# Layer 3's key tiles taken two at a time in one stream across blocks, with one mask product on GpSimd

## Chip, cores and metric

One core of one Trainium2 chip. The metric is the device time of one execution in microseconds (us), lower is better.

## The reference, cut to what matters

Four residual layers on a tensor of 4 images, 256 channels, 48 x 48 pixels. The change touches the last one only, a linear attention over three box windows (half sizes 24, 12 and 6 pixels):

```python
    def _L3_conv_ref(x, Wq, Wk, Wv, Wout, bout):      # HEADS = 8, WINDOWS = (1, 2, 4)
        ...
        q = jax.nn.sigmoid(q)
        k = jax.nn.sigmoid(k)
        v = v / jnp.maximum(jnp.linalg.norm(v, axis=1, keepdims=True), 1e-12)
        Ik = _integral(k)
        Ikv = _integral(jnp.einsum('bfhw,bghw->bfghw', k, v))
        outs = []
        for w in WINDOWS:
            ws = Hh // w
            wk = _box(Ik, ws, Hh, Ww)
            wkv = _box(Ikv, ws, Hh, Ww)
            attn = jnp.einsum('bdhw,bdfhw->bfhw', q, wkv)
            norm = jnp.einsum('bdhw,bdhw->bhw', q, wk)
            outs.append((attn / (norm[:, None] + 1e-06)).reshape(b, C, Hh, Ww))
        o = jnp.concatenate(outs, axis=1)
        return jnp.einsum('bchw,oc->bohw', o, Wout) + bout[None, :, None, None]
    ...
    x = x + _L3_conv_ref(_gn(x), L3_conv_Wq, L3_conv_Wk, L3_conv_Wv, L3_conv_Wout, L3_conv_bout)
```

## The kernel before

The kernel computes this as masked attention without a softmax. A **block** is one image, one pair of heads and 8 rows of queries (384 of them); there are 96. A **key tile** is 8 rows by 16 columns of keys; a block sees 12 to 18, in all 1440. For each tile TensorE makes the scores of both heads (two matmuls). For each of the three windows the scores are multiplied by a mask (VectorE; ScalarE copies the part where the mask is all ones) and TensorE adds them, times the values, to that window's sum. Such a **product** is one matmul call for each of the two heads, their 64-column weights side by side in the array, so that the heads can run at once; the trace shows each call as two instructions. Image 0's q, k and v are projected ahead of the stream of tiles; those of images 1 to 3 are dealt out between tiles by `background()`, as are the output projections.

```python
        def attend(b, ct, rb, pr, qs, background):
            accs = [ps_acc.tile(...) for wi in range(NW)]       # one PSUM buffer per window
            ...
            ahead = scores(*tiles[0])
            for i, (a, c) in enumerate(tiles):
                s = ahead
                if i + 1 < len(tiles):
                    ahead = scores(*tiles[i + 1])
                for wi in reversed(range(NW)):
                    if (a, c) not in todo[wi]:
                        continue
                    ...
                    for p0, p1, masked in pieces:               # the copied piece first, then the sides
                        if masked:
                            nc.vector.tensor_mul(dst, src, mask[wi][...])
                        else:
                            nc.scalar.copy(dst, src)
                    for j in range(2):                          # one product, head by head
                        nc.tensor.matmul(accs[wi][64 * j : 64 * (j + 1)]..., vst[pr][:, a * NKC + c, j, :],
                                         sm[:, j, 0:n, 0 : c1 - c0], start=..., stop=...)
                    if (a, c) == todo[wi][-1]:
                        nc.scalar.copy(stage[:, wi, :], accs[wi])
                background()
            ...                                                 # stores, on GpSimd's DMA queue
        ...
        for i, (b, ct, rb, pr) in enumerate(order):
            if (ct, rb, pr) == (0, 0, 0) and b + 1 < B:
                soon.append(projections(b + 1, ps_m, "st", [P, 512]))
            if i + 1 < len(order):
                qs[i + 1] = load_q(*order[i + 1])
            attend(b, ct, rb, pr, qs.pop(i), background)
            if rb == NRB - 1:                                   # the image's last blocks
                ...
                    while soon: ...                             # finish the next image's projections
                    load_kv(b + 1, 0, pr)
```

The order of instructions on an engine isn't that of this text: a scheduler decides it from the dependencies.

## Time and profile before

| | before |
|---|---|
| time, median (3 runs) | 4886.5 us (4876.69 to 4886.75) |
| span of the profiled run | 4876.6 us, mean granted clock 0.970 (the share of its full clock that TensorE was given) |
| image 0's projections, first matmul to first score of the stream | 1595.7 to 1709.7: 114.0 us |
| the stream of tiles, first score to the end of the last sum | 3124 us |
| last sum (its start) to the end | 43.3 us |
| busy over the whole span | TensorE 92%, VectorE 50%, ScalarE 22%, GpSimd 16% |

TensorE is nearly always busy, so the time is made in its own sequence: what its instructions need in this order, and where it waits. The other engines matter only by the waits they cause. The lines themselves stand in the prediction.

### The profile page before, as it was taken

What the parts mean: (1) busy time and instruction counts of PE and PEld (TensorE: products, weight loads), DVE (VectorE), ACT (ScalarE), POOL (GpSimd) and SP (SyncE); (2) the same over time, 40 slices, a digit from 0 to 9 for tenths busy, and PEclk for the clock granted to TensorE, in tenths of its full rate; (3) what the DMA queues carried; (4) which work ended last, traced back from release to release, by engine and by line L of the source; (5) the groups of instructions that cost most, each with busy time, mean ns of one, the idle gap of its engine ahead of it and who ended that gap; (6) DMA issues with size and microseconds to landing.
All of it is one profiled execution on the core that took longest, in us unless ns stands there. A gap on an engine that the chain in (4) does not pass through costs nothing.

```text
span 4876.6 us, 64267 instructions
## 1 busy us (share of the span) xinstructions
PE 4481.8 (92%) x24676; PEld 2571.1 (53%) x24676; DVE 2446.6 (50%) x5718; ACT 1088.2 (22%) x2227; POOL 756.9 (16%) x1237
## 2 busy tenths in 40 slices
PE   6999989989969699999999999999999998999997
PEld 4776967867858344444444444444444443444443
DVE  7543253253222155655555566555566565666564
ACT  0011001001010333223223322222322222322221
POOL 0000100100001732012123102212301211000111
PEclk9999999999979899999999999999999999999998
DMA  7241141141040641132252132234214225103222
GB/s 279 82 64 51 54 64 44 43 75 47 30 41 10 207 127 62 44 91 87 76 133 85 44 88 83 72 100 117 78 25 108 81 63 135 30 24 98 61 70 61
DMA packets 259252, 382.22 MB, mean 78 GB/s; under 512 B 96547, under 2 KB 207107, under 8 KB 252419
## 3 DMA queue, kind: packets, MB, share of 16 engines
q1 hardware_dynamic: 215267, 262.09, 20.1%
q0 software_dynamic: 38160, 108.02, 8.3%
q10 hardware_dynamic: 5520, 8.00, 0.5%
q8 instruction: 197, 3.23, 0.3%
q14 instruction: 108, 0.88, 0.1%
HBM read 259.50 MB, written 120.02 MB: 78 GB/s over the span
## 4 chain that ended last, share of the span: by engine, by line
PE 75%; DVE 9%; DMA 6%; issue 5%; POOL 3%; ACT 2%; SPq 1%; DVEq 0%; POOLq 0%; ACTq 0%
PE acc L1058 30%; PE s L1006 13%; PE cv L502 13%; PE cv L637 10%; DVE sm L1048 5%; PE out_ps L1120 4%; PE proj_ps L876 2%; PE ap L614 2%; POOL xn L862 1%; DVE o L1115 1%; DMA band_d<-e 1%; DMA rows<-band_d 1%; DMA nr<-n_d 1%; DVE v L458 1%; SPq L561 1%
## 5 line engine op out<-in xcount | busy, mean ns | idle before, releaser
L1048 DVE TENSOR_TENSOR sm<-s,masks 128x240 f32<-128x240 f32 (+22 forms) x4032 | 1688.5, 456 | 1118.0 <-PE s L1006 685.0
L1058 PE MATMUL acc<-sm,vst 128*64 128x320 f32 (+14 forms) x13440 | 1984.5, 398 | 122.8 <-DVE sm L1048 103.1
L1058 PEld LDWEIGHTS acc<-sm,vst 128*64 128x64 f32 x13440 | 761.7, 136 | 853.4 <-issue 405.5
L1056 ACT COPY sm<-s 128x528 f32<-128x528 f32 (+3 forms) x1440 | 690.7, 486 | 1603.3 <-DVE sm L1048 1586.7
L1006 PE MATMUL s<-qs,kst 128*128 128x320 f32 (+3 forms) x2880 | 838.0, 373 | 9.3 <-DVE sm L1048 8.6
L1006 PEld LDWEIGHTS s<-qs,kst 128*128 128x128 f32 x2880 | 435.3, 189 | 741.0 <-issue 693.1
L502 PE MATMUL cv<-v,wt 128*128 128x288 f32 x2912 | 763.4, 417 | 30.2 <-DVE v L458 21.0
L502 PEld LDWEIGHTS cv<-v,wt 128*128 128x128 f32 x2912 | 548.3, 192 | 195.6 <-issue 20.8
L637 PE MATMUL cv<-pad,wl_sb 128*128 128x384 f32 (+1 forms) x2592 | 476.8, 347 | 16.9 <-ACT pad L708 12.1
L637 PEld LDWEIGHTS cv<-pad,wl_sb 128*128 128x128 f32 x1728 | 322.6, 194 | 17.2 <-issue 12.3
L1072 POOL DMA_DIRECT2D o_d<-stage x192 | 97.0, 505 | 1314.2 <-ACT sm L1056 1059.5
L1120 PE MATMUL out_ps<-o,wout_sb 128*128 128x384 f32 x576 | 222.3, 513 | 45.2 <-DVE o L1115 44.4
L1068 ACT COPY stage<-acc 128x384 f32<-128x384 f32 x288 | 137.8, 478 | 483.4 <-PE acc L1058 477.1
L516 DVE SCALAR_TENSOR_TENSOR rows<-cv,rows 128x288 f32<-128x288 f32 x144 | 57.1, 450 | 284.2 <-PE cv L502 284.2
L1120 PEld LDWEIGHTS out_ps<-o,wout_sb 128*128 128x128 f32 x576 | 100.0, 191 | 139.4 <-DVE o L1115 66.8
L670 DVE SCALAR_TENSOR_TENSOR x<-cv,alpha,x 128x384 f32<-128x384 f32 x48 | 29.7, 618 | 224.3 <-PE cv L637 224.2
L446 POOL MEMSET v<- 128x192 f32 x28 | 8.3, 296 | 785.6 <-issue 416.5
L168 ACT ACTIVATE rsq_s<-gn_v 128x2 f32<-128x2 f32 x16 | 3.3, 204 | 561.1 <-DVE gn_v L195 561.1
L637 PEld LDWEIGHTS <-wl_sb 128*128 128x128 bf16 x864 | 85.9, 100 | 64.9 <-issue 7.7
L614 PEld LDWEIGHTS ap<-seen,xT 120*128 120x128 f32 (+2 forms) x832 | 105.6, 205 | 13.6 <-ACT seen L607 11.8
L181 DVE BATCH_NORM_STATS2 gn_st<-x 128x6 f32<-128x384 f32 x192 | 100.8, 552 | 23.7 <-DMA x<-in_x_dram 20.7
L614 PE MATMUL ap<-seen,xT 120*128 120x120 f32 (+3 forms) x832 | 109.7, 290 | 2.0 <-ACT seen L607 1.6
(145 smaller groups left out, 2197.9 us busy)
## 6 DMA issues: line engine op xcount, KB each, us to landing
qs<-q_d SPq DMA_DIRECT2D x384, 96.0 KB, 2.2
kst<-k_d SPq DMA_DIRECT2D x128, 288.0 KB, 7.8
wt<-wt SPq DMA_DIRECT2D x80, 448.0 KB, 3.9
o_d<-stage POOLq DMA_DIRECT2D x192, 144.0 KB, 2.3
o<-o_d POOLq DMA_DIRECT2D x24, 1152.0 KB, 5.7
rc<-r_d POOLq DMA_DIRECT2D x192, 144.0 KB, 3.6
q_d<-hl SPq DMA_DIRECT2D x48, 384.0 KB, 2.7
k_d<-hl SPq DMA_DIRECT2D x48, 384.0 KB, 2.5
```

The costliest lines, as they stand in the source:

```text
L181: nc.vector.bn_stats(st[:, ct, s, :], xt[:, ct, s * RB : (s + 1) * RB, :])
L502: nc.tensor.matmul(pss[half], wt[:, ct, k, :], vt[:, ct, :, t0 : t0 + NTH, k : k + HP], start=((part, ct, k) == (0, 0, 0)), stop=((part, c ...
L614: nc.tensor.matmul(pf[:, f, a:e], xTs[k + i][:n, f, mo * P : (mo + 1) * P], seen[:n, 1 + i, a:e], start=(i == 0), stop=(i == near[-1]),)
L637: nc.tensor.matmul(ps, w_sb[:, ct, t, mo * P : (mo + 1) * P], pad[:, ct, r0 : r0 + RB, c0 : c0 + W], start=(n == 0), stop=(n == len(parts) ...
L876: nc.tensor.matmul(ps, proj[name][:, ct, mo * P : (mo + 1) * P], xn[:, ct], start=(ct == 0), stop=(ct == NCT - 1),)
L1006: nc.tensor.matmul(s[:, j, 0 : (r1 - r0) * (c1 - c0)], kst[2 * pr + j][:, a * NKC + c, :], qs[:, j, r0:r1, c0:c1], start=True, stop=True,)
L1048: nc.vector.tensor_mul(dst, src, mask[wi][:, mr : mr + n, mc : mc + p1 - p0] .unsqueeze(1) .to_broadcast([P, 2, n, p1 - p0]),)
L1056: nc.scalar.copy(dst, src)
L1058: nc.tensor.matmul(accs[wi][64 * j : 64 * (j + 1)].rearrange("p (r w) -> p r w", w=W)[:, r0:r1, c0:c1], vst[pr][:, a * NKC + c, j, :], sm[ ...
L1068: nc.scalar.copy(stage[:, wi, :], accs[wi])
L1072: nc.gpsimd.dma_start(out=o_d[b][rb, h * D : (h + 1) * D, :], in_=stage[64 * j : 64 * j + D].rearrange("p w n -> p (w n)"),)
L1120: nc.tensor.matmul(ps, wout_sb[:, kt, mo * P : (mo + 1) * P], t["o"][:, kt % NCT, kt // NCT, :], start=(kt == 0), stop=(kt == NW * NCT - 1),)
```

## The change

Its intent, as its few words say: two tiles at a time, in one stream that does not stop between blocks, so that scores come four in a row and TensorE changes less often between scores and sums; ScalarE's copies first; and the third window's mask product, where its columns lie within ScalarE's copy, on GpSimd, which multiplies that copy by the mask. GpSimd is mostly emptied for this: its elementwise work in the projections goes to VectorE and ScalarE, but for the squares of v, and its DMA issues go to SyncE. Core of the diff (the same moves of other DMA issues and the rearranged bodies of `scores` and `sums` are cut):

```diff
-        tc.tile_pool(name="smp", bufs=7) as smp,
+        tc.tile_pool(name="smp", bufs=12) as smp,
@@ projections
-                        nc.gpsimd.tensor_scalar(
+                        nc.vector.tensor_scalar(
                             xn[:, ct]...
-                    nc.gpsimd.tensor_copy(hl[:, 0], t)
-                    nc.gpsimd.tensor_sub(hl[:, 1], t, hl[:, 0].bitcast(F32))
+                    nc.scalar.copy(hl[:, 0], t)
+                    nc.vector.tensor_sub(hl[:, 1], t, hl[:, 0].bitcast(F32))
-                    nc.gpsimd.tensor_mul(
+                    nc.vector.tensor_mul(
                         vt[:, :, :, 0:D], ...
@@ mask products
-                for wi in reversed(range(NW)):
+                for wi in (0, 1, 2):
...
+                    if wi == 0 and abs(a - rb) * RB + RB <= h:
+                        f0, f1 = max(0, c * KC + KC - h), min(W, c * KC + h + 1)
+                        nc.scalar.copy(sm[:, :, 0:n, f0 - c0 : f1 - c0], s[...])
+                        copied = sm, r0, c0, f0, f1
+                        pieces = [(c0, f0), (f1, c1)]
...
+                        if wi == NW - 1 and copied and copied[3] <= p0 and p1 <= copied[4]:
+                            big, br, bc = copied[:3]
+                            src = big[:, :, r0 - br : r1 - br, p0 - bc : p1 - bc]
+                            nc.gpsimd.tensor_mul(dst, src, m)
                         else:
+                            nc.vector.tensor_mul(dst, src, m)
@@ stores, finish()
-                nc.gpsimd.dma_start(
+                nc.sync.dma_start(
@@ the stream
-            attend(b, ct, rb, pr, qs.pop(i), background)
+        def take(batch):
+            got = []
+            for i, a, c, last in batch:
+                if i not in blocks:
+                    begun(i)                       # next image's projections appended to soon
+                got.append(blocks[i].scores(a, c))
+            return [blocks[i].masked(a, c, s) for (i, a, c, last), s in zip(batch, got)]
+        def add(batch, sms):
+            for i in sorted({e[0] for e in batch}):
+                for wi in (1, 0, 2):
+                    for (n, a, c, last), sm in zip(batch, sms):
+                        if n == i and wi in sm:
+                            blocks[i].sums(wi, a, c, *sm[wi])
+            for i, a, c, last in batch:
+                if last:
+                    done(i)                        # at an image's end: run(soon), load_kv
+                background()
+        batches = [stream[n : n + 2] for n in range(0, len(stream), 2)]
+        ahead = take(batches[0])
+        for n, batch in enumerate(batches):
+            sms = ahead
+            if n + 1 < len(batches):
+                ahead = take(batches[n + 1])
+            add(batch, sms)
```

## The prediction

Written before the changed kernel had run. ("Batch" in it is an image where projections are meant, and a pair of tiles elsewhere.)

> **What bounds the kernel now.** I read the page first, then a table by stage, then the waits of layer 3, then the timeline of one block. The table by stage gives, for three stretches, busy time by engine:
>
> ```profile
> core 0: us, PE busy (x) PEld busy (x) DVE busy (x) ACT busy (x) POOL busy (x), PEclk, DMA share, GB/s
> 1596.00:1709.00 113.00, 77.89 (x199) 44.41 (x199) 19.86 (x58) 39.27 (x69) 85.73 (x99) 0.80 0.63 203
> 1710.00:4833.00 3123.00, 2963.74 (x17343) 1363.20 (x17341) 1816.42 (x4324) 903.53 (x1897) 579.00 (x936) 0.99 0.28 78
> 4833.00:4877.00 44.00, 11.63 (x28) 5.50 (x28) 4.75 (x6) 0.48 (x1) 8.73 (x17) 0.65 0.28 80
> ```
>
> Everything the diff touches lies in these 3280 us; the 1596 us before them stay. The first stretch is the projections of batch 0, with GpSimd the busiest engine. The second is the attention stream: 1440 key tiles in 96 blocks, TensorE busy 95%, VectorE 58%. The third is the tail. So TensorE bounds the stream, and its own pace must be taken apart. In the timeline of TensorE (start, duration, engine, line, operation, count), at the end of one block and the start of the next:
>
> ```profile
> 3616.81 0.56 PE L1006 MATMUL s<-qs,kst 128*128 128x320 f32 x2
> 3617.30 0.76 PE L1058 MATMUL acc<-sm,vst 128*64 128x320 f32 x4
> 3617.99 0.62 PE L1006 MATMUL s<-qs,kst 128*128 128x384 f32 x2
> 3618.54 0.76 PE L1058 MATMUL acc<-sm,vst 128*64 128x320 f32 x4
> 3619.23 0.56 PE L1006 MATMUL s<-qs,kst 128*128 128x320 f32 x2
> 3619.72 0.87 PE L1058 MATMUL acc<-sm,vst 128*64 128x384 f32 x4
> 3621.07 1.98 PE L1058 MATMUL acc<-sm,vst 128*64 128x384 f32 x11 [0.48 <-DVE sm L1048]
> ```
>
> From start to start: two score matmuls of 320 columns take 0.49 us, of 384 columns 0.55, so 0.42 ns a column plus 0.11 to 0.12 us each. One product (four instructions: two passes for each of the two heads, whose 64-column weights lie side by side, so the heads run at once) takes 0.69 us for 320 columns. Single starts in the same trace show each pass at 0.83 ns a column, 0.267 us here, so 2 x 0.267 = 0.53 us are streaming, and 0.156 us come once per run of products: 0.054 at its first product, 0.102 at the change back to scores. The last line is the start of a block: 1.35 us after the product before it, of which only about 0.75 are that product. And this run has six instructions, not four or eight:
>
> ```profile
> 3628.20 1.38 PE L1058 MATMUL acc<-sm,vst 128*64 128x312 f32 x6
> 3629.52 0.42 PE L1006 MATMUL s<-qs,kst 128*128 128x320 f32 x1
> ```
>
> It holds one head of a 312-column product and both heads of a 384-column one. It takes 1.32 us; with the 312-column half counted at half a product it would be 0.64 + 0.26 + 0.156 = 1.06. The missing 0.26 us is one pass of 312 columns: a head alone leaves half the array idle. I call a product whose two heads are parted by other work torn; with its two halves it costs two passes extra, 1.67 ns a column.
>
> Who waits in the stream (engine and line, what for, total us, times, longest):
>
> ```profile
> PEld acc L1058 <- DVE sm L1048: 317.1, 898, 7.9
> PE acc L1058 <- DVE sm L1048: 103.1, 195, 7.7
> DVE sm L1048 <- PE s L1006: 685.0, 993, 3.2
> DVE sm L1048 <- ACT sm L1056: 412.8, 895, 2.0
> ```
>
> TensorE waits for masked products in small pieces, while VectorE waits for TensorE and ScalarE: a round trip, not a full engine.
>
> **What the Trainium skill says.** "TensorEngine Tiling (Array Packing)", Key Properties: tiles operate independently, and changing the tiling mode drains the engine. The trace agrees: two 64-column heads stream together, and each change between scores and products costs about 0.1 us. "PSUM — Partial Sum Buffer", The four PSUM rules: GpSimd cannot reach PSUM; hence its new product reads ScalarE's copy, and has that copy ahead of it. "GPSIMD Engine Reference", Elementwise: two-input operations take about twice VectorE's time. Here GpSimd took 611 ns for 256 elements and 1479 for 768, VectorE 419 and 957 on the mask products: 1.5 times. "SBUF — State Buffer", SBUF: two separate sides: a VectorE instruction with two SBUF inputs and a GpSimd one that reads SBUF exclude each other. The mask products have one input in PSUM, so the page's condition spares them; no run yet shows it.
>
> **The change, part by part.** The changed program's static order can be counted beside the old one's; both have 2880 score matmuls and 3360 products.
>
> Floor of the stream before, in us: products 858,400 columns x 1.667 ns = 1431; scores 970,752 x 0.417 ns = 405, and 2880 x 0.115 = 331; 1655 runs of products x 0.156 = 258; projections and output projections 313; entering and leaving them 330 x 0.1 = 33; between their own matmuls 30; 113 torn products, 29,390 columns x 1.667 = 49. Sum 2850. The stretch took 3123, so 273 us are waits.
>
> After: the first three terms, the 313 and the 30 stay. Runs of products fall to 1091: 170 (-88). Projections stand in fewer, longer groups: 108 x 0.1 = 11 (-22). But torn products rise to 487 with 147,731 columns: 246 (+197), because the scores of a second tile are put between the heads of a product. Sum 2937, **87 us more than before**. Pairing the tiles saves less in changes than the tearing costs.
>
> So the gain has to come out of the 273 us of waits. VectorE's mask products go from 4032 to 3072 and from 1.172 to 1.024 million elements; at 155 ns + 1.045 ns an element (from the mean durations by shape) that is 1849 to 1546 us. It gains 48 normalisations, 96 subtractions and 24 scalings, about 95 us. ScalarE loses 288 copies of 294 ns and gains 96 of 480. GpSimd gains 672 products of 282 elements on average, by the two durations above about 0.65 us, 440 us in all, and loses casts, subtractions, normalisations and its DMA issues. No engine comes near TensorE. In the middle of a block, two tiles need about 3.9 us of TensorE against 2.2 of VectorE and at most 1.8 of GpSimd, and their products are used a batch later: I expect hardly a wait there.
>
> Waits I expect to remain:
> - At the start of a block the new first-window sums follow the old ones directly in 50 of 95 cases, and share the accumulator; ScalarE's copy (478 ns) and two hand-overs lie between. About 0.65 us there and 0.4 elsewhere: 50 us.
> - Projections of batches 2 and 3 (84 matmuls each) no longer lie one by one between tiles; they stand in bursts around the first blocks of the batch, with one PSUM buffer. The profile shows such a pair waiting 0.94 us for ScalarE's sigmoid (the x4 group at 2717.54). Forty-two pairs at about 0.8 us, 2 bursts: 70 us.
> - Output projections waiting for VectorE's division products, 24 times about 2 us: 45. Ends of blocks, where VectorE masks 640 or 768 elements a tile against 1.2 us of TensorE: 25. First loads and the rest: 10.
>
> Sum 200, against 273. Stream: 2937 + 200 = 3137, 14 more than before.
>
> Projections of batch 0: GpSimd's 85.7 us leave nearly whole. TensorE needs about 9 us a row block and ScalarE 8 with its two table loads of 1.28, against 16 now; the first 17 us wait for weights in any case. I take 27 us off. The tail keeps its chain of transfers.
>
> Bottom-up: 4886 + 14 - 27 = 4873. The remaining waits are guesses on the high side more than the low (block starts and output projections may lie beside each other), so I put the centre 35 us lower, at **4838 us**.
>
> **The rivals.** (1) The waits vanish nearly wholly: the batch gives VectorE and GpSimd so much lead that only the bursts stay. For it: idle time on every other engine. Then 2937 + 80 in the stream, about 4725 us. (2) The copy-to-GpSimd chain becomes the new wait: 0.51 + 0.65 us after the scores, used a batch later, so against it; but if GpSimd's product with a broadcast bf16 mask took 1.3 us, two of them would fill most of a batch, and the time would be about 4980. (3) The transfers, all on one queue now, come late: stores wait there for ScalarE in front of the next loads of q. Loads are issued a block (some 30 us) ahead, so I expect nothing but a few us after the bursts; if not, 30 to 60 us more, about 4920.
>
> **Range and chances.** The floor is counted, with perhaps 25 us of error; the waits are 200 with 60 either way, the first stretch 15. That makes 4740 to 4930 for 8 in 10. Faster by over 2% means below 4789: 0.28. Slower by over 2% means above 4984: 0.06. Within: 0.66.
>
> **What would show it.** Right: runs of six or ten product instructions much more frequent in TensorE's timeline; fewer changes; TensorE's waits for VectorE down by more than half; projections of batches 2 and 3 in two clumps with ScalarE as the releaser; GpSimd products near 0.65 us; the first stretch near 85 us. Wrong: if torn heads cost nothing (the two heads of different products filling each other's gaps), the stream would come out over 100 us shorter; if products wait for GpSimd, the waits will name it.

## The result, and the profile after

| | before | after |
|---|---|---|
| time, median | 4886.62 us (4876.69 to 4891.39, 4 runs) | 4740.72 us (4731.44 to 4746.84, 4 runs) |
| ratio | | 0.9702, 95% interval 0.9677 to 0.9727 |
| span of the profiled run, clock | 4876.6, 0.970 | 4744.7, 0.959 |
| image 0's projections | 114.0 | 93.4 |
| the stream | 3124 | 3006 |
| last sum to the end | 43.3 | 42.8 |

Faster by 3.0%. All outputs are right. Ratios here are the mean time of one kernel's fast runs over that of the other's of the same rounds, so not quite the ratio of the quoted medians. In the profiles the stream gave 118 us and the projections of image 0 gave 21; the unchanged layers ahead took 7 us longer (1595.7 and 1602.6 us to the first projection).

The table by stage of the kernel after (for each stretch: its length, then busy time and instructions by engine, then TensorE's granted clock, DMA share and GB/s):

```profile
core 0: us, PE busy (x) PEld busy (x) DVE busy (x) ACT busy (x) POOL busy (x), PEclk, DMA share, GB/s
1603.00:1696.00 93.00, 71.84 (x200) 39.19 (x200) 43.51 (x108) 52.24 (x96) 17.00 (x27) 0.87 0.83 265
1696.00:4700.00 3004.00, 2876.14 (x17310) 1645.61 (x17310) 1576.12 (x3482) 847.92 (x1678) 544.75 (x740) 0.97 0.29 81
```

GpSimd's work in the first stretch fell from 85.7 us to 17.0. In the stream VectorE lost 240 us. TensorE is still 96% busy.

Its waits there, with VectorE's for ScalarE (engine and line, what for, total us, times, longest; PEld is TensorE's load of weights, acc a sum, stage ScalarE's copy of a finished one):

```profile
DVE sm L1058 <- ACT sm L1035: 1032.5, 778, 6.4
PEld s L1003 <- DVE sm L1058: 102.1, 182, 0.6
PEld acc L1070 <- ACT stage L1080: 66.0, 69, 1.1
PE acc L1070 <- DVE sm L1058: 16.4, 14, 3.2
PEld acc L1070 <- DVE sm L1058: 14.5, 14, 3.5
PEld acc L1070 <- POOL sm L1055: 5.7, 32, 0.2
```

The sums' wait for VectorE (317.1 and 103.1 us before) is nearly gone, and hardly a product waits for GpSimd. At block starts new sums wait for the copy of the old ones (66.0 us of weight loads), as the prediction listed. TensorE's timeline:

```profile
3563.32 0.56 PE L1003 MATMUL s<-qs,kst 128*128 128x320 f32 x2
3563.81 0.58 PE L1070 MATMUL acc<-sm,vst 128*64 128x216 f32 x2
3564.32 0.56 PE L1003 MATMUL s<-qs,kst 128*128 128x320 f32 x2
3564.82 2.85 PE L1070 MATMUL acc<-sm,vst 128*64 128x216 f32 x22
...
3595.20 0.87 PE L1003 MATMUL s<-qs,kst 128*128 128x320 f32 x4
3595.99 2.74 PE L1070 MATMUL acc<-sm,vst 128*64 128x216 f32 x24
```

Two things are to be seen. The x2 and x22 groups of sums hold an odd number of heads: one head of a 216-column product was cut off by the next scores (torn). And four scores in a row take 3595.99 - 3595.20 = 0.79 us, less than twice the 0.49 of a group of two: 0.53 us of it are streaming (4 x 320 columns at 0.417 ns), so the four change over in 0.26 us, against 2 x 0.22.

GpSimd's product on the page (busy us, mean ns, then its idle time):

```profile
L1055 POOL TENSOR_TENSOR sm<-sm,masks 128x352 f32<-128x352 f32 (+7 forms) x672 | 501.5, 752 | 2081.5 <-ACT sm L1035 1964.3
```

752 ns, against the predicted 650. GpSimd is busy for 544.75 of the stream's 3004 us, so over four fifths of it stay idle.

**The account.** To compare kernels I divided TensorE's stream into terms from start-to-start intervals in the traces. Streaming is columns at 0.417 ns (scores) or 1.667 ns (products); it is 405 and 1431 us in every kernel. The stream ends with its last sum, so the wait of the last output projection behind it (17 to 20 us of the tail in five of these kernels) is in no term. "Score turnover" is what a score matmul takes beyond streaming; where that is over 150 ns, 115 count as turnover and the rest as "score waits". "Changes" are 156 ns a run of products. Of what is left of a run, the idle gaps are "sum waits"; the rest goes to "torn heads" in runs with an odd number of heads and to "rest of whole runs" otherwise. Projections and output projections are what they take beyond streaming. "Lost clock" is the sum of (1 - granted clock) x time between 1700 and 4380 us, good to about 2 us; it is no further term, as its cost lies within the others. The projections' small negative values are the error of this division. All in us:

| term | before | after | spread | order_sums | spread_order | order_one | zeros |
|---|---|---|---|---|---|---|---|
| score turnover | 318 | 254 | 250 | 206 | 207 | 329 | 208 |
| score waits | 47 | 57 | 65 | 81 | 83 | 157 | 75 |
| changes | 258 | 170 | 175 | 117 | 112 | 225 | 112 |
| torn heads | 62 | 176 | 175 | 10 | 0 | 0 | 0 |
| sum waits | 113 | 32 | 20 | 106 | 128 | 47 | 107 |
| rest of whole runs | 121 | 64 | 49 | 65 | 48 | 16 | 33 |
| projections of images 1 to 3 | 40 | 113 | 14 | 98 | 7 | -17 | -10 |
| output projections | 24 | 8 | 7 | 18 | 41 | 34 | 51 |
| stream | 3124 | 3006 | 2889 | 2842 | 2776 | 2941 | 2726 |
| lost clock | 27 | 77 | 23 | 113 | 73 | 35 | 68 |

### The profile page after: what moved, and what is told of

Its sections match the earlier page's. It is cut to its first block, busy times and chain, and to the rows that moved or that the text cites. A ratio compares the mean times of both kernels' runs of the same rounds, so it can differ in the third digit from the quotient of the medians.

```text
span 4744.7 us, 63732 instructions
## 1 busy us (share of the span) xinstructions
PE 4406.4 (93%) x24676; PEld 2859.1 (60%) x24676; DVE 2232.7 (47%) x4926; ACT 1045.0 (22%) x2035; POOL 640.6 (14%) x949
## 4 chain that ended last, share of the span: by engine, by line
PE 86%; DMA 4%; DVE 4%; ACT 2%; issue 1%; SPq 1%; POOL 0%; ACTq 0%; DVEq 0%; POOLq 0%
PE acc L1070 38%; PE s L1003 13%; PE cv L502 13%; PE cv L637 10%; PE out_ps L1145 4%; PE proj_ps L876 3%; PE ap L614 2%; PE proj_ps L915 2%; DMA band_d<-e 1%; DMA rows<-band_d 1%; DVE v L458 1%; SPq L561 1%; ACT sg L893 1%; DMA w_raw<-in_w_dram 1%; DVE sm L1058 1%
## 5 line engine op out<-in xcount | busy, mean ns | idle before, releaser
L1070 PE MATMUL acc<-sm,vst 128*64 128x320 f32 (+16 forms) x13440 | 1915.1, 389 | 59.6 <-ACT stage L1080 23.1
L1058 DVE TENSOR_TENSOR sm<-s,masks 128x128 f32<-128x128 f32 (+14 forms) x3072 | 1366.5, 499 | 1143.7 <-ACT sm L1035 1032.5
L1070 PEld LDWEIGHTS acc<-sm,vst 128*64 128x64 f32 x13440 | 1008.6, 137 | 721.7 <-issue 395.4
L1035 ACT COPY sm<-s 128x528 f32<-128x528 f32 (+2 forms) x1152 | 590.0, 535 | 1401.3 <-PE s L1003 1361.5
L1055 POOL TENSOR_TENSOR sm<-sm,masks 128x352 f32<-128x352 f32 (+7 forms) x672 | 501.5, 752 | 2081.5 <-ACT sm L1035 1964.3
L1003 PE MATMUL s<-qs,kst 128*128 128x320 f32 (+3 forms) x2880 | 751.4, 363 | 6.9 <-DVE sm L1058 6.2
L1003 PEld LDWEIGHTS s<-qs,kst 128*128 128x128 f32 x2880 | 447.9, 190 | 399.6 <-issue 188.1
L1145 PE MATMUL out_ps<-o,wout_sb 128*128 128x384 f32 x576 | 207.4, 504 | 22.1 <-DVE o L1140 18.2
L876 PE MATMUL proj_ps<-xn,wq_sb 128*128 128x384 f32 x192 | 87.8, 590 | 35.4 <-ACT sg L893 20.5
L876 PE MATMUL proj_ps<-xn,wk_sb 128*128 128x384 f32 x192 | 93.4, 616 | 27.0 <-ACT sg L893 25.8
```

What stands on the lines that cost most here:

```text
L876: nc.tensor.matmul(ps, proj[name][:, ct, mo * P : (mo + 1) * P], xn[:, ct], start=(ct == 0), stop=(ct == NCT - 1),)
L1003: nc.tensor.matmul(s[:, j, 0 : (r1 - r0) * (c1 - c0)], kst[2 * pr + j][:, a * NKC + c, :], self.qs[:, j, r0:r1, c0:c1], start=True, stop=True,
L1035: nc.scalar.copy(sm[:, :, 0:n, f0 - c0 : f1 - c0], s[:, :, r0 - sr : r1 - sr, f0 - sc : f1 - sc],)
L1055: nc.gpsimd.tensor_mul(dst, src, m)
L1058: nc.vector.tensor_mul(dst, src, m)
L1070: nc.tensor.matmul(acc[64 * j : 64 * (j + 1)].rearrange("p (r w) -> p r w", w=W)[:, rows[0] : rows[1], cols[0] : cols[1]], vst[pr][:, a * ...
```

## The experiments

**My theory after the result.** The stream came out 131 us shorter than predicted because two terms of its floor were mis-sized (torn heads, and the turnover of scores in groups of four), while the waits fell about as predicted. The rival: the torn heads cost what I said or are even useful, and it is the waits that vanished. A second question is where the gain comes from: the pairing, the GpSimd product, or the side moves. Three calls were made; a kernel is compared with the kernel before in the same call (its medians there: 4894, 4906 and 4897 us), and kernels of different calls by these ratios.

**Projections without bursts: spread.** In the change, `take` runs one pair ahead, so the next image's first block is begun, and the projections of the image after it are put on the list, just before the old image's last block ends and empties the whole list. So all 84 projection matmuls are issued at once, twice. The edit empties the list only up to the image that is needed:

```diff
-                soon.append(projections(b + 1, ps_m, "st", [P, 512]))
+                soon.append((b + 1, projections(b + 1, ps_m, "st", [P, 512])))
-                    run(soon)
+                    run(b + 1)          # only entries with soon[0][0] <= b + 1
```

> The changed kernel with one repair: at the end of a batch only the projections of the next batch are drained, not those of the batch after it, so that no burst of 84 projection matmuls stands in the stream (longest group 6 instead of 34; torn products 471 against 487, runs of products 1119 against 1091). Theory: the bursts cost what projections take beyond their streaming, 112 us in the changed trace against 40 before, plus the dips of the granted clock that go with the idle time: the time falls by 60 to 90 us, to about 4665. Rival: the work of the projections has to be done somewhere and the burst only moves it; the time stays within 15 us of 4741.

Measured: 4625.89 us (4616.46 to 4633.44), 0.9455 of before (0.9437 to 0.9472), 2.5% less than the change (0.9455 / 0.9702), about 120 us and more than the 60 to 90 expected; the rival, that the burst only moves the work, falls. In TensorE's timeline of the kernel after, a stretch of the first burst:

```profile
2505.12 2.07 PE L876 MATMUL proj_ps<-xn,wq_sb 128*128 128x384 f32 x4 [2.31 <-ACT sg L893]
2507.76 2.93 PE L876 MATMUL proj_ps<-xn,wk_sb 128*128 128x384 f32 x4 [0.58 <-ACT sg L893]
2511.27 2.93 PE L876 MATMUL proj_ps<-xn,wk_sb 128*128 128x384 f32 x4 [0.58 <-ACT sg L893]
```

and the table by stage over it, in the kernel after and then in spread:

```profile
2459.00:2499.00 40.00, 26.81 (x83) 13.25 (x79) 15.28 (x36) 20.34 (x39) 5.77 (x9) 1.00 0.67 225
2499.00:2545.00 46.00, 33.94 (x65) 16.18 (x64) 16.85 (x41) 18.95 (x35) 7.18 (x11) 0.63 0.46 156
```

```profile
2459.00:2499.00 40.00, 39.60 (x227) 23.19 (x228) 21.71 (x45) 10.16 (x21) 6.51 (x9) 1.00 0.41 116
2499.00:2545.00 46.00, 45.88 (x310) 26.51 (x308) 27.88 (x66) 16.41 (x33) 9.41 (x14) 1.00 0.22 67
```

In the burst TensorE finishes 65 matmuls in 46 us, in spread 310. A group of four projection matmuls (two calls) waits for ScalarE's sigmoid to free the one PSUM buffer, 0.46 to 0.58 us each and 2.31 where ScalarE loads tables. Then the granted clock falls to 0.50 for 34.1 us, and the same group takes 2.93 us instead of 1.56. The second burst has two such dips. The Trainium skill, "TensorE: Matmul & The Clock Gate", Part 1, says that the array's clock is halved after about an idle window of 3.4 us and restored after a busy one. The trace agrees that idling halves it, but here no single wait between matmuls was above 2.4 us. So a burst costs twice, by its waits and by the clock (lost clock 77 to 23 us).

**The order held: order_sums and spread_order.** Score and sum matmuls get an order dependency on the one traced before (no wait; it only binds the scheduler), so both heads of a product stay together. spread_order is spread with this order for scores, sums and both kinds of projections.

```diff
-                    nc.tensor.matmul(...)            # in scores and sums
+                    in_order(nc.tensor.matmul(...))  # not before the matmul traced last
```

> The changed kernel with TensorE's scores and sums forced into the order in which the program writes them (order only, no wait added): torn products 27 instead of 487, groups of four scores 667 instead of 368, runs of products 747 instead of 1091; bursts of projections stay. Theory (torn heads and short groups cost time): 176 us for torn heads, 54 us of changes and about 60 us of score turnover leave; but scores are no longer put in early, so waits at block starts come back with up to 160 us: 100 to 200 us faster, about 4590. Rival: the scheduler's tearing fills waits that exist anyway; then the forced order gives nothing or costs, 4730 to 4800.

> Both: no bursts, and every TensorE instruction of the stream in the program's order: no torn product, 718 groups of four scores, 720 runs. Theory: the two savings add, about 4520. Rival of the torn heads: like the kernel with the bursts removed alone or slower.

Measured: order_sums 4569.48 us (4555.34 to 4583.71), 0.9341 (0.9317 to 0.9364); spread_order 4503.20 us (4498.13 to 4508.34), 0.9203 (0.9188 to 0.9218). The torn products fall from 487 to 27 and to none, and their cost from 176 us to 10 and 0. The waits of sums rise in exchange, from 20 to 128 us between spread and spread_order. The timeline of TensorE in spread_order:

```profile
3389.49 3.37 PE L1084 MATMUL acc<-sm,vst 128*64 128x384 f32 x24
3392.78 0.86 PE L1017 MATMUL s<-qs,kst 128*128 128x320 f32 x4
3393.58 2.85 PE L1084 MATMUL acc<-sm,vst 128*64 128x216 f32 x24
3396.36 0.91 PE L1017 MATMUL s<-qs,kst 128*128 128x384 f32 x4
```

Now every group is four scores and then whole products. So a torn head does cost, against the rival; but the risen waits suggest that the scheduler tore products where TensorE would have waited for a mask product, and that part of what tearing costs was saved there. Net, the order is worth 2.7% on top of spread (0.9203 / 0.9455). Spread and order_sums aren't additive: the bursts stay in order_sums (98 us of projections, lost clock 113).

**The GpSimd product taken back: mask_dve and order_mask_dve.** VectorE does all mask products, in the change and in spread_order.

```diff
-                        if wi == NW - 1 and copied and copied[3] <= p0 and p1 <= copied[4]:
+                        if False:
```

> The changed kernel with the third window's masked product back on VectorE, reading the scores (GpSimd has none). VectorE rises from 47 to about 53% busy, so as a matter of work nothing should happen. But the order then has 1113 torn products with 328,000 columns (487 with 148,000), 1296 runs, 174 groups of four. Theory (the static order sets TensorE's pace): 200 to 300 us slower, 4940 to 5040, for the order alone. Rival (GpSimd's product counts by relieving VectorE): 0 to 40 us slower.

> The repaired and ordered kernel with the third window's product on VectorE instead of GpSimd; TensorE's order is the same by force. Theory (the large loss of the unordered kernel with this edit came from its static order): VectorE gets 672 products of about 0.45 us, 300 us of work, but has idle time for it in the middle of blocks; 20 to 80 us slower, 4520 to 4580. Rival (GpSimd's product was needed for VectorE's sake): the loss of 188 us that the edit showed without forced order comes again.

Measured: mask_dve 4929.09 us (4923.31 to 4935.24), 1.0076 of before (1.0061 to 1.0091), 3.9% slower than the change, just under the range expected, and 0.8% slower than the kernel before. order_mask_dve 4595.57 us (4586.83 to 4600.36), 0.9378 (0.9359 to 0.9396), 1.9% slower than spread_order. In mask_dve the scheduler answers the later mask products by taking scores forward: 1113 torn products instead of 487, groups of four scores in 174 places instead of 368, torn heads 246 us, changes 202, score turnover 292. With the order fixed the same 672 products cost half of that, as waits: score waits go from 83 to 140 us, because VectorE holds the two score buffers longer. My range there (4520 to 4580) was too low. So the GpSimd product is a working part, worth 1.9 to 3.9% according to what the scheduler makes of its absence.

**Tiles one at a time: order_one.** spread_order with single tiles instead of pairs.

```diff
-        batches = [stream[n : n + 2] for n in range(0, len(stream), 2)]
+        batches = [stream[n : n + 1] for n in range(len(stream))]
```

> The repaired and ordered kernel (no bursts, TensorE in program order, 4503 us) with one key tile at a time instead of two, nothing torn in either: 1439 runs of products instead of 720 and 1438 groups of two scores instead of 718 of four. Theory (changes and turnover): 719 more changes of 0.156 us are 112 us, and 1440 third and fourth scores lose their hidden turnover of about 0.09 us, 110 us more; waits about as now: 200 to 240 us slower, 4700 to 4745. Rival (pairing matters for the lead that it gives VectorE): waits grow on top, 4800 and more. Rival (pairing is worth nothing once nothing is torn): 4500 to 4550.

Measured: 4680.51 us (4676.07 to 4687.75), 0.9549 (0.9532 to 0.9567), 3.8% slower than spread_order, a little less than expected. Changes double (112 to 225 us, 720 runs to 1439), which is what pairing was meant for. The score turnover grows as well, 207 to 329 us, as I expected before this run but not in the prediction: in a group of four the first score takes about 120 ns beyond streaming and the last 108, but the two in the middle 16 and 15; in groups of two both take the full amount. Without pairs sums wait less (128 to 47 us).

**The parts alone in the kernel before: before_moves and before_order.** before_moves has only the moved elementwise work and DMA issues; before_order only the bound order of scores and sums.

```diff
# before_moves
-                        nc.gpsimd.tensor_scalar(xn[:, ct]...      +  nc.vector.tensor_scalar(...)
-                    nc.gpsimd.tensor_copy(hl[:, 0], t)            +  nc.scalar.copy(...)
-                    nc.gpsimd.tensor_sub / tensor_mul             +  nc.vector.tensor_sub / tensor_mul
-                    nc.gpsimd.dma_start (stores, finish)          +  nc.sync.dma_start
# before_order
-                        nc.tensor.matmul(...)                     +  in_order(nc.tensor.matmul(...))
```

> The kernel before with only the side moves of the change: normalisation, subtraction and scaling from GpSimd to VectorE, the cast to ScalarE, all of the third layer's stores and loads to the SyncE queue. The stream's order is nearly the old one (117 torn, 1646 runs). Theory: only the projections of batch 0 gain, 15 to 25 us, 4860 to 4880. Rival (freeing GpSimd's queue shortens the chain of divisions and stores): 40 us and more.

> The kernel before with scores and sums forced into program order: torn products 6 instead of 113. Theory: 62 us of torn-head time and 12 of changes leave, some waits come back: 20 to 60 us faster, 4830 to 4875. Rival (torn heads fill waits): the same or slower.

Measured: before_moves 4820.85 us (4815.21 to 4824.03), 0.9833 (0.9817 to 0.9849), about 82 us where my theory said 15 to 25 and the rival 40 or more. By the profiles image 0's projections give 28 of it, the tail 8, and the stream 41. The long waits of the kernel before show where the last come from. At one of them its timeline of all engines has

```profile
2496.09 0.57 POOL L1088 DMA_DIRECT2D nr<-n_d  x1
2505.24 0.20 DVE L1089 TENSOR_SCALAR nr<-nr 128x72 f32<-128x72 f32 x1 [5.68 <-DMA nr<-n_d]
2506.39 0.94 PE L1058 MATMUL acc<-sm,vst 128*64 128x117 f32 x8 [5.24 <-DVE sm L1048]
```

VectorE stood 5.68 us before the norms `nr`; the mask products behind that came late, and TensorE stood 5.24 us. GpSimd had issued the load of `nr` late: it had itself stood 7.51 us until a store of the norms had landed, and it issued the larger load of `o` first. There are three such places, each at the end of an image (TensorE stands 5.0 to 7.7 us) and each with a dip of the clock. In before_moves VectorE waits there 0, 0 and 0.55 us for `nr`, and the same row of waits has no long one:

```profile
PEld acc L1058 <- DVE sm L1048: 268.7, 858, 1.9
```

(317.1, 898, 7.9 before.) The lost clock falls from 27 to 9 us. Which of the moves cures this, the other queue or the emptier GpSimd, isn't separated. before_order: 4980.16 us (4972.02 to 4998.62), 1.0164 (1.0137 to 1.0192), slower, against the 20 to 60 us gain that I expected. The torn heads do go (62 to 4 us), but the waits of sums rise from 113 to 210 us and those of scores from 47 to 96. In that kernel the scheduler's tearing and early scores filled waits, as the rival had it. So in these runs a fixed order pays in the changed kernel and not in the one before; that it needs mask products in time is my reading.

**The order of the windows: order_rev_dve and one_first.** order_rev_dve is order_mask_dve with the windows third, second, first, as in the kernel before, so that ScalarE's copy comes last. one_first is spread_order with the second window ahead of the copy.

```diff
-                for wi in (0, 1, 2):
+                for wi in (2, 1, 0):        # order_rev_dve;  (1, 0, 2) in one_first
```

> order_mask_dve (all mask products on VectorE, order fixed, projections spread: 4595.6 us) with the windows taken third, second, first, as in the kernel before, so that ScalarE's copy no longer stands ahead of VectorE's products. Theory (copies first buy little by themselves, because sums are used a batch later; what VectorE does first is what matters, and with the copy first VectorE waits for it in 487 places, 725 us of idle time that the trace of order_mask_dve shows): same or a little faster, 4550 to 4600. Rival (ScalarE's copies first is a working part: the copy gives the score buffer back late otherwise, and the first window's sums wait): 4620 to 4680.

> spread_order (4503 us) with the windows taken second, first, third: VectorE does the second window's product from the scores while ScalarE copies, then the first window's sides, and GpSimd's product follows the copy as before. If VectorE's wait for the copy (841 us, 545 times in spread_order, idle time off TensorE's path in the middle of a block, but on it at a block's start) is part of the remaining block-start waits of about 170 us, this takes 20 to 50 us: 4455 to 4485. Rival: the block-start waits are VectorE's throughput (two products of 768 elements), then no change: 4495 to 4510.

Measured: order_rev_dve 4606.89 us (4597.08 to 4612.52), 0.9398 (0.9367 to 0.9429), just above my range, and not told apart from order_mask_dve (0.9378, 0.9359 to 0.9396): without the GpSimd product, copies first or last make no difference that these runs resolve. one_first 4677.47 us (4674.34 to 4679.43), 0.9548 (0.9523 to 0.9573): 3.7% slower than spread_order, where both theories had said equal or faster. The waits, in spread_order and then in one_first:

```profile
DVE sm L1072 <- ACT sm L1049: 864.6, 550, 16.7
```

```profile
ACT sm L1049 <- DVE sm L1072: 1409.6, 886, 19.2
DVE sm L1072 <- ACT sm L1049: 453.0, 776, 1.2
```

ScalarE and VectorE take turns at one score tile, in the order of the program, though both only read it. The Trainium skill, "PSUM — Partial Sum Buffer", Terms, gives a likely reason: two engines on the same bank and partitions at once are an error, "reads against reads included". The waits agree. With the copy first it can run while VectorE is at the tile before; put behind a VectorE product, every tile has the chain VectorE, ScalarE, VectorE. At a block start that lies on TensorE's path: around the scores of a block's third and fourth tile TensorE stands idle for 143 us in spread_order and 212 in one_first. In its timeline of one_first:

```profile
2102.78 1.16 PE L1084 MATMUL acc<-sm,vst 128*64 128x280 f32 x8
2105.77 0.53 PE L1017 MATMUL s<-qs,kst 128*128 128x320 f32 x2 [1.83 <-DVE sm L1072]
2107.28 0.98 PE L1017 MATMUL s<-qs,kst 128*128 128x384 f32 x2 [0.98 <-DVE sm L1072]
2108.19 5.80 PE L1084 MATMUL acc<-sm,vst 128*64 128x384 f32 x24
```

TensorE waits 1.83 us, the clock is halved from 2106.3 to 2113.1 us, and a second wait, 0.98 us, begins as it falls: the 24 product matmuls take 5.80 us instead of the 3.37 that the same group takes in spread_order above. The lost clock is 137 us in one_first, 73 in spread_order. Score waits (83 to 180 us) and the rest of whole runs (48 to 106) hold most of the loss.

**Fewer elements at a block's start: zeros and zeros_one_first.** Most of the remaining waits of spread_order lie at block starts (TensorE is idle for 200 us of the stream, 143 of them around the scores of a block's third and fourth tile). The first tile of a block is masked over the whole width, so that the sum buffers are written everywhere. In zeros GpSimd writes the masked-out columns as zeros and VectorE multiplies the rest. zeros_one_first adds the window order of one_first.

```diff
+                    for z0, z1 in ((c0, v0), (v1, c1)):          # v0, v1: columns that the window sees
+                        if z0 < z1:
+                            nc.gpsimd.memset(sm[:, :, 0:n, z0 - c0 : z1 - c0], 0.0)
-                    pieces = [(c0, c1)]
+                    pieces = [(v0, v1)]
```

> spread_order with the masked-out columns of a block's first tile (9 of 48 in the second window, 21 in the third) written as zeros by GpSimd instead of multiplied by VectorE: 480 elements less for VectorE in each of 96 blocks, about 0.5 us each at 1.045 ns an element. If the waits at block starts are VectorE's throughput: 30 to 48 us less, 4455 to 4475. Rival (they are the chain through ScalarE's copy, or GpSimd's zeros come late and take their place): 4495 to 4530.

> Both edits together. If the two act on the same wait: no better than the better one of them, 4450 to 4470. If on different ones, the sum: 4410 to 4450.

Measured: zeros 4460.09 us (4457.54 to 4463.11), 0.9105 (0.9081 to 0.9129), 1.1% less than spread_order, as expected. zeros_one_first 4471.66 us (4465.99 to 4474.92), 0.9127 (0.9102 to 0.9152): no better than zeros. The loss of one_first nearly vanishes with the zeros, so the two act at the same place, the block starts (143 us of idle time there in spread_order, 106 in zeros). That the window order costs 3.7% without the zeros and next to nothing with them fits the clock (lost clock 58 us with, 137 without: shorter waits at block starts no longer halve it), but I haven't separated the two causes by a run. zeros is the best version found: 8.9% faster than the kernel before, 6.2% faster than the change.

## Why the prediction was wrong

It gave "within 2%" two chances in three; the kernel was 3.0% faster, at the very edge of the range.

- **Streaming, changes: right.** 405 and 1431 us are the same in all kernels, and the 1091 runs are at 170 us; runs with whole products still take 156 ns beyond streaming with one product, 161 with two and 181 with six, in the median.
- **Torn heads: the step that failed first.** "Torn products rise to 487 with 147,731 columns: 246 (+197)". They did rise to 487, but cost 176 us, against 62 before (+114). I had charged two passes extra for each, one for each half, from one torn half measured once (0.26 us). The charge for a lone half was right, the number of lone halves wasn't: 487 torn products have 974 halves, and the trace has 687 runs of products with one lone half (an odd number of heads of one width), which cost one pass each (in the median 1.03 times its columns at 0.833 ns), and 23 with two of different widths. The other 241 stand in runs that hold an even number of heads of every width, and these show no excess (178 ns beyond streaming in the median): there two halves of one width can run side by side. In order_sums, with 27 torn products left, the term is 10 us, so it is measured and not just what is left over.
- **Turnover of scores: the second.** "After: the first three terms ... stay", so 331 us. It fell to 254: in groups of four the two middle scores take about 15 ns instead of 115. Such groups were in the trace of the kernel before (22 of its 1424 groups); I averaged over them. order_one, without pairs, is back at 329, which shows the cause.
- **The floor's sign was therefore wrong.** With 176 for 246 and 254 for 331 the floor after is 2937 - 70 - 77 = 2790, 60 less than before, where the prediction had 87 more.
- **Waits: right in sum.** 200 predicted; what is left of the measured 3006 above that floor is 216. The parts agree less than the sum, which is partly luck: output projections take 8 us beyond streaming, where 45 were to be waits, while the waits of scores and sums and the rest of whole runs come to 153, where the list had 85. The bursts were foreseen and their size (70) agrees with the projections' term (+73), but their whole effect by taking them out is 2.5% or about 120 us, because of the halved clock and of the waits of neighbours.
- **Rival 1 came closest in time (4725) for the wrong reason.** The waits did not vanish; the floor was lower. Its own terms give 4753 (4886 - 106 in the stream - 27), so 4725 was also a slip. The sign that I had named for free torn heads, a stream over 100 us shorter, came (131) although they are not free: a single total can't tell the terms apart.
- **GpSimd's product: right in kind, 752 ns for 650.** No wait for it appears. What I did not see is how much depends on it: without it the change is slower than the kernel before.
- **Side moves: undervalued.** I gave them 27 us, in image 0's projections (21 measured). before_moves shows about 82 us in the kernel before, half of it in the stream, where three long waits behind a late load go. They stood in the profile (7.9 and 7.7 as the longest waits) and I had filed them under 273 us of small pieces. How much of this carries into the change can't be read off, since the parts aren't additive.
- **Tail: right**, 43.3 and 42.8.

## What to carry to other kernels

Before you charge a cost per event, measure it on several events in their neighbourhoods: a torn half that meets another of its width, and the middle ones of four scores, cost much less than the same thing alone. When work is issued ahead in a program, look at every queue that the "ahead" step fills: here it emptied a list of background work at once, and the cost was 2.5%. Where TensorE is the bound, count short waits that come close together as more than their length, because a halved clock may follow: here 1.4 to 2.0 us of idle time within 3.413 us could be enough.

## What the Trainium skill lacked or had wrong

- "TensorEngine Tiling (Array Packing)", Key Properties: the drain at a change of mode agrees (0.156 us a run of products). It lacks that in a row of four score matmuls in one mode the turnover is about 120, 16, 15 and 108 ns beyond streaming, so that the middle ones are nearly hidden.
- The same page lacks what parting two column tiles costs: 487 torn products cost 176 us, about 0.36 us each (a lone half costs one pass, 0.833 ns a column), and a bound order takes that to zero.
- "GPSIMD Engine Reference", Elementwise: twice VectorE's time for two inputs; here 752 ns at 282 elements on average, against 450 ns that VectorE would take by 155 + 1.045 ns an element (an estimate from its durations): 1.67 times.
- "TensorE: Matmul & The Clock Gate", Part 1: a clock halved after an idle window of about 3.4 us. In the streams of the 14 traces every change of the clock lies on a grid of 3.413 us, one for each trace, to within 5 ns, so the length agrees; but the window need not be idle throughout. The windows ahead of the 342 falls held 1.39 to 3.41 us without a matmul; every window at full clock with over 2.02 us was followed by half clock, and none with under 1.39. In one_first one wait of 1.83 us sufficed, and the half clock lasted 6.8 us; in the bursts, with matmuls running for most of the time, it lasted 34.1 us.
- "PSUM — Partial Sum Buffer", Terms: the exclusion of two readers agrees. No page says what the order of the readers costs: a copy put behind one of VectorE's products and ahead of GpSimd's cost 3.7% (one_first), and a copy put last, with no GpSimd product waiting for it, nothing that the runs resolve (order_rev_dve).
